# A graph network on one core: the convolutions of the last three or four target tiles are summed by gathers on Pool and adds on VectorE instead of by products with the adjacency table

## The chip, the cores and the metric

The kernel runs on one core of a Trainium2 chip. A time is the microseconds of one execution on the device. The engines of the core work side by side, each through its own queue of instructions, in the order of that queue: PE (matrix products), DVE (VectorE), ACT (ScalarE), POOL (GpSimd) and SP, which here only issues transfers. ACT and Pool issue transfers as well. An engine that must wait for another holds everything behind it in its queue.

## The reference

3125 nodes with 256 features and 50000 edges, sorted by target, pass through four blocks, each "x = x + layer(layernorm(x))" twice. What matters here are the two plain graph convolutions, the one of block 2 (three layers) and the one of block 3 (one layer):

```
def gcn_layer(h, src, dst, norm, n, W, b):          # block 2, with an edge from each node to itself
    h = h @ W
    msg = h[src] * norm[:, None]
    agg = segment_sum(msg, dst, num_segments=n)
    return agg + b
h = relu(gcn_layer(x, ..., W1, b1))
h = relu(gcn_layer(h, ..., W2, b2))
h = gcn_layer(h, ..., W3, b3)
...
h = x @ W                                            # block 3, one layer, no such edges
out = segment_sum(h[src] * norm[:, None], dst, num_segments=N)
```

with norm = d(src)^-1/2 · d(dst)^-1/2 and d the in-degree. After each convolution comes a mixture of 8 experts, of which every node takes the 2 best (hidden sizes 1024 in block 2, 512 in block 3). Blocks 0 and 1 are attention convolutions over the same edges, an expert stage and a recurrence with gates.

## The kernel before, in words

Nodes are cut into 25 tiles of 128 (NP = 3200 rows, the last ones empty); a node sits on a partition and its 256 features beside each other, and `x` stays on the core. Early in the program the edges are turned into a table of counts in DRAM, `ct16` [128, 25, 3200]: how often source row s·128+p has an edge to each target column. A convolution is then a dense product: for a group of target tiles (a span), SP loads the table's columns of these targets (`table_columns`, L814, tiles named `c`, three buffers), Pool adds the identity to the blocks on the diagonal where the layer has edges from each node to itself (L828, "own"), and PE multiplies, over all 25 source tiles, the source's rows by these columns.

The rows, `hs`, are f32 rows times d(src)^-1/2, cut into three bf16 parts (high, mid, low) so that three products with bf16 counts keep the precision. `parted` (L840) makes them, two tiles at a time: Pool casts (L847), DVE subtracts (L848), Pool casts (L849), DVE subtracts (L850).

`gcn` (L1585) runs a whole convolution. The first two layers of block 2 use `convolve` (L1529): 7 spans of 4, 4, 3, 4, 3, 4, 3 tiles, each 25 sources × 2 halves of the features × 3 parts = 150 matmuls (L1540), features on partitions and targets along the free axis, accumulated over two banks of PSUM, with two sets of banks. When a span ends, `done` runs: DVE multiplies the two banks by the targets' factor (`agg`, L1663), ACT applies bias and relu (L1664), PE multiplies each tile by the next layer's weights (L369, 4 matmuls a tile), ACT scales the result into `new` (L1656), and `parted` writes the next layer's `hs`. In PE's queue these products stand 9 matmuls into the next span.

The last layer of block 2 and the single layer of block 3 use `convolve_rows` (L1546): 13 spans of at most two tiles, rows of targets on partitions, for each tile and source one matmul 512 wide (high and mid, L1560) and one 256 wide (low, L1564). `done` here is `add`: DVE adds the scaled sums to `x` (L1684). Each finished span then passes through the front of the experts (`Experts.front`, L2198): normed rows on DVE, transposes and router product on PE, choice of two experts and places on DVE, and sends of the rows to the experts' slots by Pool (L2344, indirect transfers). These pieces are spread over the matmuls of the following spans by lags that are written out in `ready`, counted in tile-steps. When the convolution has ended, `Experts.run` (L2606) computes the experts; weights of the coming turn (`first`, L2599) are loaded by SP, `ahead` of them before the run starts.

The order in which instructions of different engines stand in the queues is not written out by hand: a scheduler places them from the order of the calls and its own view of when each can start. The order within a queue is fixed when the program is built.

Other names used below: `put_rows` (L834) stores rows of a tile in DRAM with a transfer issued by ACT; `even_spans` (L69) cuts a number of tiles into spans of nearly equal size; `recurrence` begins with a projection of all steps (L1801 with `px`, and DVE's L1824), about 66 us long, before the steps themselves. Attention convolutions gather rows with indirect transfers by Pool (L2019). If a flag is raised (`flags`), a general program runs after the normal one.

Of the kernel before, what the change touches and what calls it, by code (L numbers as in the profile page):

```python
# [19 lines left out]
P = 128  # L20
# [35 lines left out]
PARTS = 3  # L56
SKIP = 20
TOL = 2.0**-16
EPS = 1e-5
# [16 lines left out]
class Net:  # L76
    def __init__(self, ctx, tc, w, out):
# [11 lines left out]

        self.flags = const.tile([1, 7], F32, name="flags")  # L90
        nc.vector.memset(self.flags, 0.0)
# [30 lines left out]
        for g in range(QUAD):  # L122
            nc.vector.memset(self.quarter[g * GROUP : (g + 1) * GROUP, g : g + 1], 1.0)
        self.turned = dram.tile([GROUPED, MANY * P], BF16, name="turned")
        self.scored = [
            dram.tile([NP, D + 2 * nh], F32, name=f"scored{i}") for i, nh in enumerate((NH, NH, 1))
# [246 lines left out]
    def edges_by_window(self, ctx, c, keep):  # L373
# [10 lines left out]
        psum = self.pool(ctx, "tabps", 2, space=PSUM)  # L384
        dram = self.pool(ctx, "tabdram", 1, space=DRAM)
        edges = self.w["edges"]
# [3 lines left out]
        )  # L390
        runs = dram.tile([RUNS, 2 * P], I32, name="runs")
        nc.sync.dma_start(
# [178 lines left out]
    def count_degrees(self, ctx, c, psum):  # L571
# [53 lines left out]

        return [lambda q0=q0: some(q0) for q0 in range(0, HALF, quarter)] + [sums]

    def on_all_partitions(self, to, col, psum):
# [899 lines left out]

    def convolve(self, cpool, accp, loops, hs, done):  # L1529

        wide = 4
        for t0, n in even_spans(wide):
            cols = self.table_columns(cpool, t0, n, wide * P, loops)
            acc = [accp.tile([P, wide * P], F32, name=f"acc{f}") for f in range(KD)]
            for s in range(NT):
                parts = self.parts(hs, s)
                for f in range(KD):
                    for i, part in enumerate(parts):
                        lhs = part[:, f * P : (f + 1) * P]
                        self.nc.tensor.matmul(  # L1540
                            acc[f][:, : n * P], lhs, cols[s], start=(s == 0 and i == 0),
                            stop=(s == NT - 1), skip_group_check=True,
                        )
            done(t0, n, acc)

    def convolve_rows(self, cpool, accp, loops, hs, done, ready, loads):  # L1546

        nc = self.nc
        wide = 2
        step, waiting = 0, []  # L1550
        for t0, n in spans(wide):
            cols = self.table_columns(cpool, t0, n, wide * P, loops, few=4 * GRP // wide)
            acc = [accp.tile([P, 4 * P], F32, name=f"acc{t}") for t in range(n)]
            def add(t, lhs, s, start=False, stop=False):

                if len(hs.shape) == 3:
                    return nc.tensor.matmul(
                        acc[t][:, :D], lhs, hs[:, s, :], start=start, stop=stop
                    )
                nc.tensor.matmul(  # L1560
                    acc[t], lhs, hs[:, s, 0:2, :].rearrange("p i d -> p (i d)"), start=start,
                    stop=stop, skip_group_check=True,
                )
                return nc.tensor.matmul(  # L1564
                    acc[t][:, D:], lhs, hs[:, s, 2, :], start=False, stop=stop,
                    skip_group_check=True,
                )

            for s in range(NT):
                for t in range(n):  # L1570
                    add(t, cols[s][:, t * P : (t + 1) * P], s, s == 0, s == NT - 1)
                step += n
                while loads and loads[0][0] <= step:
                    with self.tc.issue_after(self.last_columns):
                        loads.pop(0)[1]()
                while waiting and waiting[0][0] <= step:
                    waiting.pop(0)[1]()
            for t in range(n):
                done(t0 + t, [acc[t][:, i * D : (i + 1) * D] for i in range(len(hs.shape) - 2)])
            for lag, piece in ready(t0, n):  # L1580
                waiting.append((step + lag, piece))
            waiting.sort(key=lambda entry: entry[0])
        return [piece for _, piece in loads + waiting]

    def gcn(self, name, weights, biases, loops, experts, split=True):  # L1585
# [3 lines left out]
        with ExitStack() as ctx:  # L1589
# [6 lines left out]
            accp = self.pool(held, name + "acc", 2, space=PSUM)  # L1596
            shape, kind = ([P, NT, PARTS, D], BF16) if split else ([P, NT, D], F32)
            inner = held.enter_context(ExitStack())
            wk = self.pool(inner, name + "work", 3)
            fresh = self.pool(inner, name + "fresh", 2)  # L1600
            lefts = self.pool(inner, name + "left", 2)
            if len(weights) > 1:
                other = self.pool(inner, name + "hs2", 1)
                aggs = self.pool(inner, name + "agg", 1)
            wts = [self.load_matrix(c, w, D) for w in weights]
            bs = [self.load(c, b, [P, KD]) for b in biases[:-1]]
            bias = self.load_row(c, biases[-1], D) if biases else None

# [13 lines left out]

            def rows_of(to, t0, n):

                if not split:
                    return to[:, t0 : t0 + n, :], lambda: None
                new = fresh.tile([P, 4, D], F32, name="new")[:, :n, :]

                return new, lambda: self.parted(lefts, to, new, t0, n)

# [6 lines left out]
            def use(t):  # L1637
                ph = psum.tile([P, 512], F32, name="tp")
                self.product(ph[:, :D], xts[t], wts[0])
                if t % 4 == 0:  # L1640
                    xts["new"] = rows_of(hs, t, min(4, NT - t))
                new, end = xts["new"]
                nc.scalar.mul(new[:, t % 4, :], ph[:, :D], disc[:, t : t + 1])
                if t % 4 == 3 or t == NT - 1:
                    end()
# [4 lines left out]
            for i in range(len(weights) - 1):  # L1650
                after = (other, last)[i].tile(shape, kind, name="hs")

                def next_layer(t, xt, to, i=i):
                    po = psum.tile([P, 512], F32, name="tp")
                    self.product(po[:, :D], xt, wts[i + 1])
                    nc.scalar.mul(to, po[:, :D], disc[:, t : t + 1])  # L1656

                def done(t0, n, acc, i=i, after=after, next_layer=next_layer):
                    w = n * P
                    agg = aggs.tile([P, KD, 4 * P], F32, name="agg")  # L1660
                    for f in range(KD):
                        a = agg[:, f, :w]
                        nc.vector.tensor_mul(a, acc[f][:, :w], dis[:, t0 * P : t0 * P + w])  # L1663
                        nc.scalar.activation(a, a, AF.Relu, bias=bs[i][:, f : f + 1])  # L1664
                    new, end = rows_of(after, t0, n)
                    for j in range(n):
                        next_layer(t0 + j, agg[:, :, j * P : (j + 1) * P], new[:, j, :])
                    end()
                    if i == 0:
                        some = x[:, t0 : t0 + n, :]  # L1670
                        nc.vector.tensor_add(
                            some, some, bias.unsqueeze(1).to_broadcast([P, n, D])
                        )

                self.convolve(cpool, accp, loops, hs, done)
                hs = after
# [16 lines left out]
            def ready(t0, n):  # L1693
                pieces = experts.front(psum, t0, n)
                if t0 + n == NT - 1:
                    lags = [1] + [16 + j for j in range(n)] + [20, 23, 25]
                else:
                    lags = [2] + [34 + 4 * j for j in range(n)] + [46, 58, 70]
                lags += lags[-1:] * (len(pieces) - len(lags))
                if t0 + n == CERTAIN:  # L1700
                    lags[-1] += 32
                return zip(lags, pieces)

            rest = self.convolve_rows(cpool, accp, loops, hs, add, ready, loads)
            held.close()
# [58 lines left out]
    def recurrence(self, name, general=False, turned=None):  # L1764
# [23 lines left out]
        with ExitStack() as ctx:  # L1788
# [18 lines left out]
            with ExitStack() as inner:  # L1807
                psz = self.pool(inner, name + "projpz", 4, space=PSUM)
                if xt is None:
# [4 lines left out]
                    for t in range(NT):  # L1814
                        xn = wk.tile([P, D], F32, name="xn")
                        self.normed(xn, x, stats, t)
                        self.transposed(psum, xt[:, :, t * P : (t + 1) * P], xn)
                steps = xt[:, :, :T].rearrange("p k (b g s) -> p k g s b", g=G, s=L)
                for g in range(G):
                    for s in range(L):  # L1820
                        pz = psz.tile([P, W], F32, name="px", padded_shape=[P, 512])
                        for k in range(KD):
                            quarters(pz, steps[:, k, g, s, :], us[:, k], k == 0, k == KD - 1)
                        nc.vector.tensor_add(pre[:, g, s, :], pz, bs)  # L1824
            with ExitStack() as inner:
                wk = self.pool(inner, name + "work", 3)
# [125 lines left out]
class GatheredAttention:  # L1952
# [143 lines left out]
    def end(self, t, state):  # L2096
        nh = self.nh
        acc = state["acc"][:, : D + 2 * nh].rearrange("p (h c) -> p h c", h=nh)
        for i, piece in enumerate(self.done(t, acc)):
            self.waiting.append((self.now + 4.0 * (i + 1), piece))  # L2100
        self.waiting.sort(key=lambda entry: entry[0])


# [660 lines left out]
def last_blocks(net, name):  # L2764

    with ExitStack() as part:
        f2 = Experts(
            net, part, "f2" + name, 1024, "L2_ffn_Wr", "L2_ffn_W1", "L2_ffn_b1", "L2_ffn_W2",
            "L2_ffn_b2", bias="L2_ffn_br", gain="L2_ffn_ln_g", shift="L2_ffn_ln_b",
            store=True, early=6, ahead=2, more=3,  # L2770
        )
# [40 lines left out]
def gnn_ffn_kernel(ctx: ExitStack, tc: tile.TileContext, w, out: bass.AP):  # L2812
    net = Net(ctx, tc, w, out)
    nc = tc.nc
    with ExitStack() as part:
        f0 = first_experts(net, part, "f0", early=10, ahead=1, more=4, late=3, rows=10)
        f0.run(rest=net.gnn0(f0))
    with ExitStack() as part:
        net.recurrence("l", turned=net.gnn1(part))
# [76 lines left out]
```

## Time and profile before

| what | value |
|---|---|
| median of 10 runs | 3951.31 us (3943.26 to 3958.70) |
| profiled execution, its own time | 3950.82 us |
| span of its trace | 3949.0 us, 71651 instructions |
| mean granted PE clock | 0.933 of full; 1.00 in the convolutions |
| PE busy | 3506.2 us, 89% of the span |
| convolutions of block 2, first two layers | 2325 to 2811 us; PE's idle time in 2330 to 2811 is 6.4 us |
| third layer of block 2 | 2811 to 3040 us |
| convolution of block 3 | 3480 to 3704 us |
| matmuls L1540 | 2100, 408.2 us |
| matmuls L1560 and L1564 | 1250 each, 411.3 and 340.8 us (they overlap) |

In lines of the profile, a time is the busy time in us, then the mean in ns, then the idle time of the engine ahead of such instructions with what ended it ("<-"). In a timeline the columns are the start, the length, and in brackets the idle time before and its releaser. PE's matmuls are pipelined, so lengths of neighbours overlap, and the step from one to the next is what counts. "L369" is the line of a helper that many products share; the names of the tiles tell them apart.

### The profile page before, as it was taken

The page shows a single profiled execution, that of the slowest core. Times are in us where ns is not written, and L with a number is a line of the kernel's source. Part 1 is how long each engine was busy: PE and PEld are TensorE (multiplying, and loading weights), DVE is VectorE, ACT ScalarE, POOL GpSimd, SP SyncE. Part 2 cuts the span into 40 slices and gives each one's busy share as a digit, 9 for nine tenths or more (in the row PEclk, how much of TensorE's full clock was granted, in tenths as well). Part 3 has the DMA queues.
Part 4 walks back from the last instruction along what each step waited for, and adds up shares of the span by engine and source line. Part 5 has one row for each costly group of instructions (what it writes and reads, how often), then busy time and mean ns, then how long its engine had stood idle before and what let it go on. Part 6 is the DMA issues. An engine that isn't in the chain of part 4 may idle for free. (4 is left out here: it accounts for less than half of the span.)

```text
span 3949.0 us, 71651 instructions
## 1 busy us (share of the span) xinstructions
PE 3506.2 (89%) x26079; PEld 2127.8 (54%) x26079; DVE 2155.4 (55%) x7897; ACT 1183.6 (30%) x3591; POOL 1422.8 (36%) x1321
## 2 busy tenths in 40 slices
PE   4777986867988798999999989999999999899897
PEld 3343222742322576744544555555566888766686
DVE  7777988547777575676766771111266211244411
ACT  2566334342343122133433450000001222320122
POOL 2778876446787474000000031111122222222243
PEclk8677988989999899999999989999999999899999
DMA  4556444644443553000000003233455344535465
GB/s 127 157 163 187 115 116 123 191 142 128 126 119 92 173 160 89 3 2 2 2 2 2 2 31 92 87 92 95 142 179 162 105 122 122 150 109 153 122 168 121
DMA packets 366366, 422.11 MB, mean 107 GB/s; under 512 B 44076, under 2 KB 320864, under 8 KB 362295
## 3 DMA queue, kind: packets, MB, share of 16 engines
q1 hardware_dynamic: 286833, 260.46, 21.9%
q0 software_dynamic: 62224, 140.41, 13.7%
q10 hardware_dynamic: 16950, 16.54, 1.3%
q8 instruction: 215, 3.52, 0.4%
q14 instruction: 144, 1.18, 0.1%
HBM read 337.37 MB, written 82.62 MB: 106 GB/s over the span
## 5 line engine op out<-in xcount | busy, mean ns | idle before, releaser
L2019 POOL DMA_INDIRECT edge<-scored,from x720 | 860.9, 1196 | 332.8 <-issue 180.1
L1560 PE MATMUL acc<-hs,c 128*128 128x512 bf16 x1250 | 411.3, 379 | 0.0
L1540 PE MATMUL acc<-c,hs 128*128 128x512 bf16 (+1 forms) x2100 | 408.2, 357 | 0.2 <-POOL hs L847 0.2
L1801 PE MATMUL pz<-lstm_v,hist 128*32 128x192 f32 x7120 | 384.2, 334 | 25.3 <-DVE hist L1902 7.0
L2685 PE MATMUL ph<-xt,first 128*128 128x256 f32 (+1 forms) x1624 | 349.2, 370 | 1.6 <-ACT xt L2651 1.0
L1564 PE MATMUL acc<-hs,c 128*128 128x256 bf16 x1250 | 340.8, 273 | 0.0
L2703 PE MATMUL py<-w,ht 128*128 x1484 | 336.2, 381 | 0.6 <-DVE y L2708 0.6
L2078 ACT ACTIVATE edge<-edge,factor 128x65 f32<-128x65 f32 (+1 forms) x960 | 251.3, 349 | 237.0 <-DVE factor L2073 220.9
L1540 PEld LDWEIGHTS <-hs 128*128 128x128 bf16 x2100 | 205.2, 98 | 199.5 <-POOL hs L847 0.6
L2685 PEld LDWEIGHTS ph<-xt,first 128*128 128x128 f32 x1624 | 290.3, 196 | 35.6 <-ACT xt L2651 1.6
L2703 PEld LDWEIGHTS py<-w,ht 128*128 128x128 f32 x1484 | 282.5, 191 | 38.3 <-issue 0.9
L1801 PEld LDWEIGHTS pz<-lstm_v,hist 128*32 128x32 f32 x7120 | 187.1, 110 | 178.6 <-DVE hist L1902 146.3
L1837 PE MATMUL pz<-pre,ident 128*128 128x192 f32 x900 | 269.4, 383 | 11.9 <-PEq L1910 11.4
L1611 POOL TENSOR_TENSOR disc<-deg,expo 128x25 f32<-128x25 f32 x1 | 4.4, 4356 | 727.4 <-DVE ends L1907 727.4
L2344 POOL DMA_INDIRECT slots<-rows,sloti x150 | 159.5, 1064 | 295.9 <-DVE rstd L345 136.5
L2693 ACT ACTIVATE ht<-ph,first 128x256 f32<-128x256 f32 (+1 forms) x406 | 160.5, 455 | 321.4 <-PE ph L2685 304.0
L976 DVE SCALAR_TENSOR_TENSOR v<-q,g1ahv,c 128x384 f32<-128x384 f32 (+1 forms) x400 | 236.8, 645 | 10.7 <-PE acc L1045 10.5
L1131 PE MATMUL acc<-g1bhv,v 128*128 128x257 f32 x850 | 206.7, 395 | 15.7 <-DVE v L976 8.5
L1837 PEld LDWEIGHTS pz<-pre,ident 128*128 128x128 f32 x900 | 136.7, 191 | 149.5 <-ACT tcell L1896 75.5
L1038 PE MATMUL acc<-v,g1ahv 128*64 128x384 f32 (+1 forms) x800 | 180.6, 560 | 28.8 <-DVE v L976 28.0
L1882 ACT ACTIVATE z<-pz 128x192 f32<-128x192 f32 x450 | 148.6, 330 | 189.7 <-PE pz L1801 175.5
L2088 PE MATMUL edgeacc<-edge,hot 128*32 128x264 f32 (+1 forms) x1440 | 141.6, 460 | 68.4 <-DVE edge L2081 34.7
(530 smaller groups left out, 5430.2 us busy)
## 6 DMA issues: line engine op xcount, KB each, us to landing
c<-ct SPq DMA_DIRECT2D x103, 640.0 KB
c<-ct SPq DMA_DIRECT2D x75, 480.0 KB
first<-in_f_first SPq DMA_DIRECT2D x29, 1158.0 KB
slots<-slots SPq DMA_DIRECT2D x159, 130.0 KB
ct<-cols SPq DMA_DIRECT2D x12, 1600.0 KB
first<-in_f_first SPq DMA_DIRECT2D x29, 642.0 KB
edge<-scored,from POOLq DMA_INDIRECT x720
first<-in_f_first SPq DMA_DIRECT2D x29, 385.0 KB
```

What stands on the lines that cost most here:

```text
L976: nc.vector.scalar_tensor_tensor(to, q[:, h, :w], hv[:, s, h, D // nh + 1 : D // nh + 2], cols[s], op0=ALU.max, op1=ALU.mult,)
L1038: made = nc.tensor.matmul(acc[h // 2][r : r + HC, :w], hv[:, s, h, :HC], v[h], start=first, stop=last, tile_position=(0, r),).ins
L1131: nc.tensor.matmul(a[:, : D + 1], v[0][:, j * P : (j + 1) * P], hv[:, s, 0, : D + 1], start=(s == 0), stop=(s == NT - 1),)
L1540: self.nc.tensor.matmul(acc[f][:, : n * P], lhs, cols[s], start=(s == 0 and i == 0), stop=(s == NT - 1), skip_group_check=True,)
L1560: nc.tensor.matmul(acc[t], lhs, hs[:, s, 0:2, :].rearrange("p i d -> p (i d)"), start=start, stop=stop, skip_group_check=True,)
L1564: return nc.tensor.matmul(acc[t][:, D:], lhs, hs[:, s, 2, :], start=False, stop=stop, skip_group_check=True,)
L1801: made = nc.tensor.matmul(pz[q * R : (q + 1) * R, :], s, m, start=start, stop=stop, tile_position=(0, q * R),)
L1837: made = nc.tensor.matmul(pz, self.ident, pre[:, g, s, :], start=True, stop=False)
L2019: nc.gpsimd.indirect_dma_start(out=tile[:, g, :], out_offset=None, in_=self.rows, in_offset=bass.IndirectOffsetOnAxis(ap=index, axis=0),)
L2078: nc.scalar.mul(part, part, factor[:, g, h : h + 1])
L2685: made = nc.tensor.matmul(ph[:, m - m0, :n, :], st["w1"][:, k * hid + m * P : k * hid + (m + 1) * P], st["xt"][:, k, :n, :], start=(k == 0 ...
L2703: nc.tensor.matmul(py[:, j, :], st["ht"][:, m, j, :], st["w2"][:, m * D : (m + 1) * D], start=(m == 0), stop=(m == nhc - 1),)
```

## The change

The last four target tiles (21 to 24; in `convolve_rows` the last three, 22 to 24) leave the dense product. `convolve` covers 21 tiles in 6 spans (4, 3, 4, 3, 4, 3) and `convolve_rows` 22 tiles in 11 spans of two. For the "near" tiles a target's edges are taken by rank: its first edge, its second, up to the 22nd. A table `ranked` holds for each target and rank the source row (or a row of zeros, if the target has fewer edges). For each rank Pool gathers, with one indirect transfer of 128 rows of 1 KB, the f32 source rows of the 128 targets; DVE adds two ranks at a time (128x512). Edges beyond rank 22, at most 128 for the four tiles together, are gathered once (`more`) and spread to their targets by one f32 product a tile with a table of ones, `beyond_hot`. The source rows lie in DRAM (`sources`, one copy for even and one for odd layers), written by `put_rows` when `new` is finished. More than 128 edges beyond the rank raise a flag.

The tables are made by `near_plan` in 16 pieces, some 70 small instructions, most on DVE, one piece after every fourth step of the recurrence's projection. The core of the diff:

```diff
+NEAR, RANKS = 4, 22
+FAR = NT - NEAR
...
+        self.sources = [dram.tile([NP + P, D], F32, name=f"sources{i}") for i in range(2)]
...
-    def convolve(self, cpool, accp, loops, hs, done):
+    def convolve(self, cpool, accp, loops, hs, done, near):
...
-        for t0, n in even_spans(wide):
+        for t0, n in even_spans(wide, FAR if near else NT):
...
+                if near:
+                    near.upto(n)
             done(t0, n, acc)
+        if near:
+            near.upto(None)
...
-        for t0, n in spans(wide):
+        for t0, n in even_spans(wide, near.first if near else NT):
...
+            for other in fronts.pop(t0 + n, ()) if near else ():
+                for lag, piece in ready(*other):
+                    waiting.append((step + 24 + lag, piece))
...
+            nears = self.pool(held, name + "near", 1) if split else None
+            gots = self.pool(held, name + "got", 5) if split else None
...
-                return new, lambda: self.parted(lefts, to, new, t0, n)
+                def end():
+                    self.put_rows(self.sources[layer % 2], new, t0, n)
+                    self.parted(lefts, to, new, t0, n)
+
+                return new, end
...
+                def near_done(t, rows, i=i, after=after, next_layer=next_layer):
+                    turned, agg = [], aggs.tile([P, KD, P], F32, name="nearagg")
+
+                    def turn():
+                        pt = psum.tile([P, KD, P], F32, name="tp", padded_shape=[P, 512 // P, P])
+                        for f in range(KD):
+                            nc.tensor.transpose(
+                                pt[:, f, :], rows[:, f * P : (f + 1) * P], self.ident
+                            )
+                        for f in range(KD):
+                            nc.scalar.activation(
+                                agg[:, f, :], pt[:, f, :], AF.Relu, bias=bs[i][:, f : f + 1]
+                            )
...
-                self.convolve(cpool, accp, loops, hs, done)
+                self.convolve(
+                    cpool, accp, loops, hs, done, near_tiles(i, FAR, 3.3, near_done)
+                )
...
-                if t0 + n == NT - 1:
+                if split and t0 + n == FAR - 1:
+                    lags = [2] + [22 + 4 * j for j in range(n)] + [34, 40, 46]
+                elif not split and t0 + n == NT - 1:
                     lags = [1] + [16 + j for j in range(n)] + [20, 23, 25]
...
-            rest = self.convolve_rows(cpool, accp, loops, hs, add, ready, loads)
+            rest = self.convolve_rows(
+                cpool, accp, loops, hs, add, ready, loads,
+                near_tiles(len(weights) - 1, FAR + 1, 3.9, near_add),
+                {12: [(FAR + 1, 2)], 18: [(FAR + 3, 1)]},
+            )
...
+                pieces = self.near_plan(inner) if turned else []
...
+                        if pieces and s % 4 == 3:
+                            pieces.pop(0)()
...
+class NearTiles:
+
+    def __init__(self, net, pool, gots, psum, rows, hs, disc, first, pace, done):
...
+        self.tiles = range(first, NT)
+        self.each = RANKS // 2
+        self.waiting, t0 = [], 7.0
+        for i, t in enumerate(self.tiles):
+            state, begin = {}, t0 + i * self.each * pace
+            self.put(begin, lambda t=t, state=state: self.begin(t, state))
+            for b in range(self.each):
+                at = begin + (b + 1) * pace
+                self.put(at, lambda t=t, b=b, state=state: self.add(t, b, state))
+            self.put(at + 0.1, lambda t=t, state=state: self.end(t, state))
+        self.more = pool.tile([P, D], F32, name="more")
+        self.gather(self.more, self.net.beyond)
+        self.fetch(5)
...
+    def fetch(self, upto):
+        for n in range(len(self.got), min(upto, len(self.tiles) * self.each)):
+            t, b = self.first + n // self.each, n % self.each
+            got = self.gots.tile([P, 2, D], F32, name="got")
+            for j in range(2):
+                r = 2 * b + j
+                self.gather(got[:, j, :], self.net.ranked[:, t - FAR, r : r + 1])
+            self.got.append(got)
+
+    def upto(self, n):
...
+        self.now += 0.325 * n
+        while self.waiting and self.waiting[0][0] <= self.now:
+            self.waiting.pop(0)[1]()
+
+    def begin(self, t, state):
...
+        nc.tensor.matmul(
+            pm[:, :D], self.net.beyond_hot[:, t - FAR, :], self.more, start=True, stop=True
+        )
...
+    def add(self, t, b, state):
+        n = (t - self.first) * self.each + b
+        if b == 0:
+            return
+        sums = state["sums"]
+        self.nc.vector.tensor_add(sums, self.got[n - 1] if b == 1 else sums, self.got[n])
+        self.fetch(n + 6)
...
-            store=True, early=6, ahead=2, more=3,
+            store=True, early=6, ahead=1, more=3,
```

`near_tiles` makes a `NearTiles` for a layer; in `upto` its pieces are called when the products written so far, at 0.325 us each, have come to their due time: the first at 7.0, then one add every 3.3 us (3.9 in `convolve_rows`). These due times order the calls; the scheduler places the instructions. `begin` also adds the tile's own three parts of `hs` where the layer has edges to itself; `end` adds the two halves of `sums` to `base` and scales; then `near_done` turns the tile, applies relu and multiplies by the next layer's weights, or `near_add` adds it to `x`. The weights of the convolutions move to a pool (`early`) that is freed before the last layer, and the second expert stage keeps one `first` load ahead where it kept two.

## Prediction

> **What bounds the kernel now.** I read the slices of the span first, to see which engine is full in the convolutions (slices 24 to 31 and 36 to 38).
>
> ```profile
> PE   4777986867988798999999989999999999899897
> DVE  7777988547777575676766771111266211244411
> POOL 2778876446787474000000031111122222222243
> PEclk8677988989999899999999989999999999899999
> ```
>
> PE is at 9 there, VectorE at 1 to 2, Pool at 1: the change moves work from the full engine to two that idle. The table of stretches says how full (columns: length, PE, weight loads, VectorE, ScalarE, Pool busy, granted clock, DMA share, GB/s); two stretches of the first two convolutions, two of the third, one of the fourth:
>
> ```profile
> 2400.00:2500.00 100.00, 99.99 (x502) 52.78 (x501) 12.84 (x19) 8.69 (x17) 10.46 (x20) 1.00 0.30 86
> 2700.00:2811.00 111.00, 110.99 (x586) 60.98 (x585) 12.59 (x19) 8.69 (x17) 12.30 (x24) 1.00 0.32 92
> 2811.00:2900.00 89.00, 88.99 (x566) 56.32 (x564) 45.02 (x262) 6.17 (x16) 17.66 (x24) 1.00 0.62 190
> 3480.00:3560.00 80.00, 80.00 (x510) 50.40 (x509) 33.60 (x156) 3.60 (x9) 16.28 (x21) 1.00 0.50 147
> ```
>
> PE never waits here, so products taken away shorten the span one for one, and a wait put on PE lengthens it one for one. The timeline shows one span's products and its handover; then the gathers that exist (groups, page):
>
> ```profile
> 2395.17 3.72 PE L369 MATMUL tp<-L_gnn_W,agg 128*128 128x256 f32 x16
> 2398.73 32.65 PE L1540 MATMUL acc<-c,hs 128*128 128x512 bf16 x152
> 2431.35 3.72 PE L369 MATMUL tp<-L_gnn_W,agg 128*128 128x256 f32 x16
> ```
>
> ```profile
> 2393.67 1.29 DVE L1663 TENSOR_TENSOR agg<-acc,dis 128x512 f32<-128x512 f32 x2 [25.78 <-PE acc L1540]
> 2398.39 0.69 DVE L848 TENSOR_TENSOR left<-new,hs 128x512 f32<-128x512 f32 x1 [3.42 <-POOL hs L847]
> ```
>
> ```profile
> L2019 POOL DMA_INDIRECT edge<-scored,from x720 | 860.9, 1196 | 332.8 <-issue 180.1
> L1560 PE MATMUL acc<-hs,c 128*128 128x512 bf16 x1250 | 411.3, 379 | 0.0
> L2344 POOL DMA_INDIRECT slots<-rows,sloti x150 | 159.5, 1064 | 295.9 <-DVE rstd L345 136.5
> ```
>
> ```profile
> 105.61 0.94 POOL L2019 DMA_INDIRECT edge<-scored,from  x1 [0.30 <-issue]
> ...
> 110.61 1.02 POOL L2019 DMA_INDIRECT edge<-scored,from  x1 [0.30 <-issue]
> ```
>
> ```profile
> 110.19 0.19 DVE L2073 TENSOR_TENSOR factor<-factor,edge 128x16 f32<-128x16 f32 x1 [3.50 <-DMA edge<-scored,from]
> ...
> 113.63 0.19 DVE L2073 TENSOR_TENSOR factor<-factor,edge 128x16 f32<-128x16 f32 x1 [1.67 <-DMA edge<-scored,from]
> ```
>
> A gather of 128 rows of 1 KB holds Pool 0.96 and the next starts 0.30 later: a step of **1.27 us** (0.95 plus 0.30 to 0.33 in the rows here; back-to-back L2019 steps have median 1.29, smallest 1.25, 95th percentile 2.26). Its rows are used 4.58 (105.61 to 110.19) and 3.02 us (110.61 to 113.63) after it started; I take 3.5.
>
> **What is removed.** A 512-wide step is 32.65 / 152 = 0.215 us, so 150 of them, one span, 32.2. Each of the first two convolutions has 25 tiles in spans 4, 4, 3, 4, 3, 4, 3 and afterwards 21 in 4, 3, 4, 3, 4, 3: one four-tile span less. The four `L369` products remain (3.72), one by one. Added on PE per tile are a 256-wide product (3.72 / 16 = 0.23) and two transposes (0.2 each at most): 0.6, times four 2.4. Net −30 each. A tile of the row-wise convolutions is 25 pairs of matmuls that start 0.326 us apart, 8.15 us; three tiles less their 0.23 each: −23.7 each. Removed: 2×30 + 2×23.7 = **107 us**. Column loads shrink too; nothing waits for them, 0.
>
> **What is added, and where it queues.** Per convolution one gather of `more`, then 22 gathers and 10 adds a tile: 89 gathers in the first two (113 us of Pool), 67 in the others (85). They would fit beside 205 us of products. But engines take instructions in order, and the changed program's order puts near work ahead of what PE needs. First convolution, counted in the built queues:
>
> ```
> Pool     more + 28 gathers, own block tile 4, 13 gathers, own 5 and 6, 13 gathers, ...
> VectorE  10 adds of tile 21, 9 of tile 22, agg of span 0 (L1904), 1 add, ...
>          next agg after 62 gathers, the third behind the cast after 81
> PE       9 products of span 1, then the L369 products of span 0
> ```
>
> So `agg` of span 0 waits for 43 gathers. The old kernel starts span 0's products at 2395.17; the last rows of `hs` exist near 2364, and a store must land before the first gather. Five bigger stores took 6.6 and 6.9 us until the following gather; I take 3.5 for one tile, so the first gather starts near 2368.5, and PE needs the products 26.6 us later. The 43rd gather starts 42×1.27 + 0.4 (own block, 31.2 / 75) ≈ 54, is usable at 58, the add takes 0.69, and products follow `agg` by 1.5 (2393.67 to 2395.17): 60.2. **PE stands 33.6.** VectorE then stands until 78.7 at tile 22's own product, which PE reaches only then; the five double buffers fill; gather 62 starts at 92.3, products go at 97.8 against PE's 89.7: 8.1 more. The third handover costs 4.7. Sum 46.4.
>
> Second convolution, same order, 44 gathers ahead, PE there at 29.7: 62.0 − 29.7 = 32.3, then 8.0, 4.7, and 0.5 for `more`: 45.5. Third (row-wise; front pieces of the experts queue on VectorE behind the adds): own block of span 1 after 15 gathers 5.5, normed rows after 32 gathers 17, selection after 44 gathers 10, the one after 62, behind eight slot sends, 8, `more` 1: 41.5. Fourth: no own blocks; normed rows after 22 gathers 7.5, selection after 42 (57.5 + 2 against 43) 16.8, the one after all 66 with eight sends between 9.5, `more` 1: 35. Stalls: **168 us**, about 286 s − 195 for a gather step of s us, since in each case the last checkpoint (81, 81, 62, 62 gathers) sets the total.
>
> Small ones. The plan of ranks adds 16 pieces to VectorE in the projection before the recurrence, where PE is full and VectorE idle in 30 of 66 us: between 0 (hidden) and 20 (every piece shown); I take 4. The second expert stage keeps one `first` load ahead instead of two: the load now starts at the convolution's end rather than 8 us ahead of its use; such loads landed in 5.7; between 0 and 8, I take 3. Stores of `sources` are 0.35 us ScalarE issues where ScalarE is 9% busy: 0, at most 2 a convolution.
>
> **Sum.** 3950.8 (profiled execution; span 3949.0; the median shown, 3951.3, is the same) − 107 + 168 + 7 = **4019 us**.
>
> [...] The gathers of this case step at 1.25 to 2.26 beside VectorE work. [...] The 704 steps have their median at 1.29, with VectorE 40 to 90% busy, so the sum stays with 1.27.
>
> **Rivals.**
> - *The gathers keep ahead (faster).* If the step is short enough, VectorE never waits and only the 107 show: 3951 − 107 + 7 = 3851. It decides at the first `agg`: 42 s + 6.1 ≤ 26.6, s ≤ 0.49; the gain ends where 286 s − 195 = 100, **s = 1.03**. Against it: no back-to-back step under 1.25 in 704. For it: those rows come from other stages and another row layout, and my walk assumes that every queued add blocks `agg`. Between 0.49 and 1.03 it ends at 3850 to 3950, say 3890.
> - *About even.* Half of the later stalls are not there (the second and third handovers, the sends), and the first ones are shorter because the first gather starts 6 us earlier: 168 − 35 − 24 = 109, 3960. Only a landing under 1 us with all later stalls gone gives within 8 us, which is 0.2%, about what can be told from no change.
> - *Worse.* Column loads (0.3 to 0.6 of the DMA engines) or the adds slow the step to 1.6: 286×0.33 = 94 more, 4113.
> - *It doesn't do what it says.* More than 128 edges beyond rank 22 would send the program to its general path. The drawn edges have 74 for the last four tiles (7159 edges, 437 targets): excluded.
>
> **Chances.** Forecast (3980 to 4060) 0.58; worse 0.14; partly refunded, 3959 to 3980, 0.07; even, within 0.2%, 0.05; faster 0.16. So slower 0.79, same 0.05, faster 0.16. The range leaves out a third of worse and nearly all of faster (0.05 + 0.14): 3935 to 4105. Bounds of the unknowns: landing 3.0 to 4.6 moves the sum by −2 to +4; steps 1.25 to 1.5, −6 to +66; first gather ±3 us, ∓12; the small ones −7 to +30.
>
> **What would show it.** In the changed profile the first two convolutions must have, some 34 us after their start, one PE gap of about 33 us ended by ScalarE or VectorE at the products of span 0, with VectorE waiting there for a gather by Pool; gathers stepping by 1.27 on Pool without pause for some 50 us; smaller gaps near the second and third handovers; and in the row-wise ones gaps of 17 and 10, and of 7 and 17, before the expert's transposes. Matmul busy time must fall by about 100. No gap at the first handover means the order did not bind; a step off 1.27 gives the total by 286 s − 195. I am wrong if PE stays full in these stages, or if gaps are ended by column loads instead.

## The result and the profile after

The changed kernel takes **4079.71 us** (median of 8 runs, 4075.52 to 4087.21), the one before 3951.26 (28 runs): a ratio of 1.0325, 95% interval 1.0316 to 1.0334. It is slower by 128 us, where 68 were forecast (4019); the direction held, and the time lies inside the range, near its upper end. In the profiled executions the span grows from 3949.0 to 4078.0.

The slices of the span of the changed kernel, rows as in those shown of before:

```profile
PE   4787886858987899999999868969699999768897
DVE  7787987457777566776676743222376211344511
POOL 2887865537884772000000164362632222363243
PEclk8777987979999999999999989979899999889999
```

PE's row of nines is broken: it is at 6 in slices 24, 27 and 29, where the three convolutions of block 2 begin, and at 7 and 6 in slices 35 and 36, where that of block 3 does. Pool is at 6 in slices 24, 27, 29 and 36, and the granted clock (PEclk) drops to 7 or 8 with PE. What PE waited for in the first two convolutions, in the third and in the fourth (the view of waits, its main lines; total us, times, longest):

```profile
PE tp L373 <- ACT agg L1905: 88.4, 8, 34.3
```

```profile
PE tp L2601 <- DVE sel L2592: 23.0, 4, 9.5
PE tp L356 <- DVE plain L2537: 14.6, 1, 14.6
PE tp L2414 <- DMA more<-sources,beyond: 4.1, 1, 4.1
PE acc L1758 <- POOL c L1022: 3.3, 1, 3.3
```

```profile
PE tp L2601 <- DVE sel L2592: 30.6, 5, 12.7
PE tp L356 <- DVE rows L2537: 15.3, 1, 15.3
```

Line 373 is the old 369, 1905 the relu behind `agg`, 2592 the choice of experts, 2537 the normed rows. The first pause in full, on PE, VectorE and Pool (timeline):

```profile
2401.69 3.35 PE L1734 MATMUL acc<-c,hs 128*128 128x512 bf16 x17
2439.39 5.51 PE L373 MATMUL tp<-L_gnn_W,agg 128*128 128x256 f32 x16 [34.34 <-ACT agg L1905]
```

```profile
2433.90 0.72 DVE L2431 TENSOR_TENSOR sums<-sums,got 128x512 f32<-128x512 f32 x1 [1.75 <-DMA got<-sources,ranked]
2437.29 0.69 DVE L2431 TENSOR_TENSOR sums<-sums,got 128x512 f32<-128x512 f32 x1 [2.67 <-DMA got<-sources,ranked]
2437.89 1.28 DVE L1904 TENSOR_TENSOR agg<-acc,dis 128x512 f32<-128x512 f32 x2
```

```profile
2432.28 0.95 POOL L2388 DMA_INDIRECT got<-sources,ranked  x1 [0.30 <-DVE sums L2431]
2433.24 0.81 POOL L1022 TENSOR_TENSOR c<-c,ident 128x128 bf16<-128x128 bf16 x2
2434.21 1.24 POOL L2388 DMA_INDIRECT got<-sources,ranked  x1 [0.16 <-issue]
```

PE stood for 34.34 us. VectorE held `agg` ready to run all that time, but had adds in front of it, each waiting 1.1 to 3.1 us for a gather (the last two are shown), and Pool issued gathers without rest but for three own blocks. This is the picture that the prediction asked for.

Sums by stage, from the same two traces. "Wait" is time in which no matmul runs; "half clock" is what matmuls of the convolutions and products lost by steps of 427 instead of 216 ns, of which more below.

| stage | before | after | change | wait | half clock |
|---|---|---|---|---|---|
| up to the first convolution | 2325.1 | 2335.5 | +10.4 | | |
| first two convolutions | 485.9 | 525.5 | +39.6 | 6.4 to 94.4 | 3.5 to 14.8 |
| third, to the experts' products | 230.1 | 267.7 | +37.6 | 2.7 to 49.0 | 0.3 to 13.2 |
| second experts' products | 380.5 | 379.1 | −1.4 | | |
| from them, with the fourth, to the next | 286.6 | 324.2 | +37.6 | 22.6 to 73.2 | 0 to 8.2 |
| third experts' products | 217.3 | 219.3 | +2.0 | | |

The half clock here is counted by steps. The profile's records of the granted clock, over the time in which PE worked, give a little more: 3.4 to 14.3, 0.4 to 14.9 and 5.0 to 14.2 us.

### The profile page after: what moved, and what is told of

Same layout as the page of the kernel before. It is cut to its first block, busy times and chain, and to the rows that moved or that the text cites. A ratio compares the mean times of both kernels' runs of the same rounds, so it can differ in the third digit from the quotient of the medians.

```text
span 4078.0 us, 71458 instructions
## 1 busy us (share of the span) xinstructions
PE 3441.6 (84%) x25545; PEld 2099.7 (51%) x25545; DVE 2276.1 (56%) x8175; ACT 1190.3 (29%) x3604; POOL 1739.7 (43%) x1640
## 5 line engine op out<-in xcount | busy, mean ns | idle before, releaser
L1758 PE MATMUL acc<-hs,c 128*128 128x512 bf16 x1100 | 383.7, 395 | 8.5 <-POOL hs L1043 5.2
L2388 POOL DMA_INDIRECT got<-sources,ranked x308 | 301.5, 979 | 154.8 <-issue 68.7
L1734 PE MATMUL acc<-c,hs 128*128 128x384 bf16 (+1 forms) x1800 | 348.8, 353 | 0.2 <-POOL hs L1041 0.2
L2337 ACT ACTIVATE edge<-edge,factor 128x65 f32<-128x65 f32 (+1 forms) x960 | 251.3, 349 | 242.4 <-DVE factor L2332 224.1
L1762 PE MATMUL acc<-hs,c 128*128 128x256 bf16 x1100 | 309.3, 281 | 0.5 <-DVE hs L1044 0.5
L1734 PEld LDWEIGHTS <-hs 128*128 128x128 bf16 x1800 | 176.4, 98 | 162.3 <-issue 1.6
L3065 POOL DMA_INDIRECT sums<-y,to x53 | 82.5, 1557 | 286.5 <-DVE y L3056 278.9
```

The source lines that it names most:

```text
L1734: self.nc.tensor.matmul(acc[f][:, : n * P], lhs, cols[s], start=(s == 0 and i == 0), stop=(s == NT - 1), skip_group_check=True,)
L1758: nc.tensor.matmul(acc[t], lhs, hs[:, s, 0:2, :].rearrange("p i d -> p (i d)"), start=start, stop=stop, skip_group_check=True,)
L1762: return nc.tensor.matmul(acc[t][:, D:], lhs, hs[:, s, 2, :], start=False, stop=stop, skip_group_check=True,)
L2337: nc.scalar.mul(part, part, factor[:, g, h : h + 1])
L2388: self.nc.gpsimd.indirect_dma_start(out=to, out_offset=None, in_=self.rows, in_offset=bass.IndirectOffsetOnAxis(ap=index, axis=0),)
```

## The experiments

The theory from the prediction: the near work costs time because of **where it stands in the queues** of VectorE and Pool; what waits for gathers holds up what PE needs. The rival: the gathers and adds cost the time **by themselves**, through traffic or engine time, in any order. A second question came from the half-clock column: what a pause of PE costs beyond its length. A time that is given without a ratio is that of one execution.

**First: held behind earlier work on VectorE.**

```diff
         while self.waiting and self.waiting[0][0] <= self.now:
-            self.waiting.pop(0)[1]()
+            self.held(self.waiting.pop(0)[1])
+
+    def held(self, piece):
+        traced, dve = self.nc.cur_bb.bb.instructions, self.nc.vector.engine
+        last = [i for i in traced[-700:] if i.engine == dve and i.name not in self.mine][-10:]
+        first = len(traced)
+        with ExitStack() as after:
+            for ins in last:
+                after.enter_context(self.net.tc.issue_after(ins))
+            piece()
+        self.mine.update(i.name for i in traced[first:])
```

> The changed kernel, with one thing added: every near piece that falls due while products are written is queued on VectorE behind the last ten VectorE instructions written before it that are not near work, so no add stands ahead of an earlier span's agg or an earlier front piece. In the built queues the first agg then stands behind 6 adds instead of 19, in the second layer behind 6 instead of 20; the gathers and adds are as many as before. Theory (order): the pauses of the changed profile, 88 us in the first two convolutions, 46 and 50 in the row-wise ones, nearly all go, and with them the stretches of half clock behind them (about 34 us of products at 427 instead of 216 ns a step): 4080 - 88 - 90 - 30 = 3870, to 3900 if the pauses at the first own block and at more stay. Rival (the work itself): 312 gathers, their traffic and the adds cost the time wherever they stand in the queue: 4050 to 4080.

Measured: 3924.93 us, ratio to before 0.9929 (0.9903 to 0.9955). The same gathers and adds, 155 us less than in the changed kernel. The rival falls. But it is 25 to 55 us short of the theory: what PE waited for in the first two convolutions is now

```profile
PE tp L373 <- ACT agg L1905: 11.7, 4, 7.4
PE acc L1734 <- POOL c L1022: 4.0, 2, 2.1
```

88.4 us have become 11.7. In the trace the longest of them comes from Pool: a cast of `hs` stands behind 16 gathers, VectorE's subtraction waits for it, and `agg` (at 2439.60) stands behind the subtraction:

```profile
2438.12 0.43 DVE L1042 TENSOR_TENSOR left<-new,hs 128x256 f32<-128x256 f32 x1 [8.77 <-POOL hs L1041]
```

**Second: adds that do not wait.**

```diff
-        self.nc.vector.tensor_add(sums, self.got[n - 1] if b == 1 else sums, self.got[n])
+        self.nc.vector.tensor_add(sums, self.still if b == 1 else sums, self.still)
```

> The changed kernel, but the adds read a tile of zeros that nothing else writes, so the sums of the near tiles leave out the gathered rows; all gathers are still made, into the same buffers, in Pool's queue as before. Theory (order on VectorE): the pauses that agg, plain and sel end go, while those that an own block on Pool ends may grow, since own blocks still stand behind 28, 40 and 41 gathers: of 184 us of pauses 100 to 160 go, 3910 to 3980. Rival (gathers slow PE by their traffic or their time on Pool, whoever waits): above 4040.

Measured: 4114.67 us, slower than the changed kernel and outside what my theory expected. Taken alone the number would speak for the rival; the waits of PE in the first two convolutions do not:

```profile
PE tp L373 <- ACT agg L1905: 80.4, 4, 46.3
PE acc L1734 <- POOL c L1022: 50.9, 4, 15.8
```

Without waiting adds the scheduler put 30 gathers in a row ahead of a cast; the own blocks (50.9 us) and the casts on Pool were late, and `agg` with them. So Pool's queue is a second place where the order binds, which I had priced only for own blocks and for single casts and sends. The experiment did not separate what it was meant to; the ninth repeats it in order.

**Third: tables alone.** `near_tiles` returns nothing and the lags are those of before:

```diff
-                ) if split else None
+                ) if False else None
```

> The changed kernel without near tiles: all 25 tiles go through the dense products with the spans and lags of before; the rank tables, the stores of the source rows and the single first load stay. It prices what is not the convolutions. My prediction had 7 us (4 for the tables, 3 for the load), the changed profile starts its first convolution 10.4 us later than the old one and ends its expert stages as early or as late within 2: 3958 to 3966. Rival (the 10 us are the scatter of one execution): within 0.2% of 3951.

Measured: 3944.00 us, ratio 0.9983 (0.9973 to 0.9994): not 7 us slower but 7 faster. Its first convolution begins 4.5 us later than before; the gain is in the stretch to the third expert stage's products (278.8 us for 286.6) and in these (211.3 for 217.3). Which part brings it (the weights' pool, the single `first` load) was not tried. Against this kernel the near tiles cost 136 us.

**Fourth: a pause of known length.** In the kernel before, PE's next span is queued behind the products of the finished one, and VectorE lengthens the handover:

```diff
+                        with self.tc.issue_after(turned) if turned else nullcontext():
...
                         nc.vector.tensor_mul(a, acc[f][:, :w], dis[:, t0 * P : t0 * P + w])
+                        for _ in range(24 if f == 0 else 0):
+                            nc.vector.tensor_scalar(a, a, 1.0, None, op0=ALU.mult)
```

> The kernel before, with PE made to pause: at each handover of a span in the first two convolutions VectorE multiplies the first half of agg 24 times by one, and PE's products of the next span are queued behind those of the finished one, which stand 0 matmuls instead of 9 into it; by the built queue 12 of 14 handovers pause. Theory (a pause of PE costs more than its length): 12 pauses of some 10 us, and behind each some 4 to 6 us of matmuls at 427 instead of 216 ns, 2 to 3 us lost each: 3951 + 120 + 30 = 4100. Rival (a pause costs its length alone): no 427 ns steps behind them and the sum of the pauses, 4070.

Measured: 4124.32 us. The first two convolutions grew by 172.7 us: 144.4 of pauses (12 of 12.0 on average, 10.6 to 12.7) and 25.8 of half clock, 2.2 for each (28.6 and 2.4 by the clock records). The timeline of the first, with the 16 matmuls behind it:

```profile
2408.30 5.16 PE L369 MATMUL tp<-L_gnn_W,agg 128*128 128x256 f32 x16 [12.50 <-ACT agg L1671]
2413.30 7.07 PE L1542 MATMUL acc<-c,hs 128*128 128x512 bf16 x32
```

The 16 took 5.16 us for the 3.72 of the kernel before. All twelve pauses show it: each, 12.0 us long on average, cost 14.2.

**Fifth: both queues held.** In addition to the first experiment, pieces are queued behind the last eight Pool instructions too, ScalarE casts, and the row-wise layers start later:

```diff
+        last += [i for i in others if i.engine == self.nc.gpsimd.engine][-8:]
...
-                    self.parted(lefts, to, new, t0, n)
+                    self.parted(lefts, to, new, t0, n, nc.scalar.copy if layer else None)
...
-        self.waiting, t0 = [], 7.0
+        self.waiting, t0 = [], 12.0 if self.adding else 7.0
...
-        self.fetch(5)
+        self.fetch(3 if self.adding else 5)
```

> The first experiment taken further: near pieces are queued behind the last ten VectorE and the last eight Pool instructions written before them that are not near work; in the first two convolutions the casts of hs for the next layer are made by ScalarE instead of Pool, so that none stands behind gathers; in the row-wise ones the first pieces fall due at 12 instead of 7 us and six gathers instead of ten are issued at once, so that the first own block stands behind 7 gathers. The first experiment left 23 us of pauses in the first two convolutions and 28 and 33 in the two others (22 of the 33 are also in the kernel before, ahead of its products), each pause ended by a cast, an own block, more or the normed rows, and 20 us of slow products. Theory (order in both queues): most of these go, 3925 - 15 - 25 - 10 = 3875, between 3860 and 3895. Rival (what is left is the time that the gathers and adds take from others): 3910 to 3930.

Measured: **3879.64 us**, ratio to before 0.9823 (0.9805 to 0.9841), the fastest version of this study. The first two convolutions take 424.3 us for 485.9, 61.6 less, with 6.1 us of waits. The products of the handover, in these two convolutions, in the changed kernel and in this one (groups):

```profile
L373 PE MATMUL tp<-L_gnn_W,agg 128*128 128x256 f32 x156 | 49.4, 481 | 88.4 <-ACT agg L1905 88.4
```

```profile
L373 PE MATMUL tp<-L_gnn_W,agg 128*128 128x256 f32 x156 | 36.7, 387 | 0.0
```

The same 156 matmuls: 88.4 us of waiting and 12.7 of half clock are gone. Whether the hold on Pool or ScalarE's casts did it, on top of the first experiment, was not tried apart. The row-wise convolutions gain little: 230.3 us, where the kernel with the tables alone has 230.5, and 274.9 for its 278.8.

**Sixth and eleventh: short pauses.** The fourth experiment without multiplications (sixth), and with 3 of them (eleventh).

> The fourth experiment without the multiplications by one: 12 handovers at which PE's next span is queued behind the products of the finished one, nothing else. There 12 pauses of 12.0 us cost 12 x 12.0 of waiting and 12 x 2.2 of products at half the clock. The multiplications took some 8.5 us of each, so 12 pauses of about 3.5 us are left. Theory (half a clock for some us follows a pause of 3.5 us as well as one of 12): 3951 + 42 + 26 = 4019. Rival (a short pause costs its length alone): 3951 + 42 = 3993.

> The sixth experiment with 3 multiplications by one. 24 of them made a pause 11.1 us longer (12.0 against 0.9), 0.46 each, so 12 pauses of about 2.3 us. Pauses of 0.9 us had no products at half the clock behind them, pauses of 3.3 us and more in the changed kernel had them for 4 to 6 us. If half the clock follows a pause of 2.3 us too: 3951 + 28 + 26 = 4005. If not: 3951 + 28 = 3979.

Measured: 3959.18 and 3990.67 us. The pauses of the sixth were 0.9 us, not 3.5 as expected, and cost their length: the two convolutions grew by 10.6 us with 10.2 more of waits, and no more half clock than before. In the eleventh, two pauses that follow one another:

```profile
2438.79 5.41 PE L369 MATMUL tp<-L_gnn_W,agg 128*128 128x256 f32 x16 [2.79 <-ACT agg L1671]
2444.03 24.54 PE L1542 MATMUL acc<-c,hs 128*128 128x384 bf16 x150
2470.93 2.86 PE L369 MATMUL tp<-L_gnn_W,agg 128*128 128x256 f32 x12 [2.35 <-ACT agg L1671]
```

16 matmuls in 5.41 us behind a pause of 2.79, 12 in 2.86 behind one of 2.35. Of its twelve pauses, three of the eight of 2.8 us had half clock behind them, none of the four of 2.35. Neither of the two expectations holds for all of them. Nor do these four set a border at 2.35 us. In the changed kernel's own fourth convolution PE works, stands for 2.29 us, works 1.7 us at the full clock and then 3.4 at half (table of stretches, columns as in the prediction):

```profile
3760.00:3762.30 2.30, 0.01 (x1) 0.00 (x0) 0.84 (x5) 0.00 (x0) 0.00 (x0) 1.00 0.06 20
3764.00:3767.40 3.40, 3.40 (x14) 1.78 (x12) 0.42 (x5) 0.63 (x2) 2.10 (x3) 0.50 0.11 39
```

A pause of 2.25 us in the same stage (at 3660.6) has none behind it, and one of 3.36 in the first experiment (at 2809.9) has none either. In the changed kernel's four convolutions all 13 pauses of 3.59 us or more have half clock in them or behind them, and so have the twelve of the fourth experiment. Of the shorter ones down to some 2 us some have it and some have not; in the first convolution of the kernel before, pauses of 2.08 and 2.10 us have it and one of 1.97 has not.

**Seventh: near tiles in the first two convolutions alone** (`near` is None in `convolve_rows`, with the lags of before).

> The fifth experiment with near tiles in the first two convolutions alone; the two row-wise ones go through all 25 tiles by products, with the lags of before. In the fifth the first two convolutions took 424 us for 486, the third 230 for 230, and the stretch from the second to the third expert stage's products 275 against 279 in the kernel with the tables alone. Theory (the row-wise convolutions give their 24 us of products back in pauses and slow products): 3944 - 61 = 3883, within 8 us of the fifth experiment's 3880. Rival (the row-wise ones do gain their 24 us each): 3880 + 48 = 3928.

Measured: 3891.70 us, ratio 0.9850 (0.9834 to 0.9867); 12 us above the fifth, where 8 were allowed and 48 would have been the rival's. The row-wise convolutions take 230.8 and 278.0 us here, 230.3 and 274.9 there, 3.6 us of the 12: their gain on PE is given back almost whole.

**Eighth: a slower pace in the row-wise layers.**

```diff
-                near_tiles(len(weights) - 1, FAR + 1, 3.9, near_add),
-                {12: [(FAR + 1, 2)], 18: [(FAR + 3, 1)]},
+                near_tiles(len(weights) - 1, FAR + 1, 4.3, near_add),
+                {14: [(FAR + 1, 2)], 18: [(FAR + 3, 1)]},
```

> The fifth experiment with the row-wise near adds due every 4.3 instead of 3.9 us, and the front of tiles 22 and 23 after the span that ends at tile 14 instead of 12. In the fifth, PE still waited there 13.5 us for sel, which stood behind adds whose gathers stood behind the sends of a span. Theory (order again: more room between gathers lets sends and gathers pass): 5 to 20 us less, 3860 to 3875. Rival (the Pool has too little time for gathers and sends in these stages in any order): 3880 or more.

Measured: 3893.64 us, 14 us slower than the fifth. The theory's 5 to 20 us of gain did not come; the third convolution waits 23.7 us instead of 20.3 and takes 236.5 instead of 230.3. A slower pace with a later front does not help; which of the two costs the time was not tried apart.

**Ninth: the second experiment in the mended order.**

> The fifth experiment, but the adds read a tile of zeros, so the gathered rows are left out of the sums while all gathers are made: the second experiment in the mended order. Theory (the second one's loss came from Pool's order, not from the gathers as such): 3945 - 61 for the first two convolutions, less 20 to 30 in the row-wise ones: 3845 to 3875. Rival (gathers cost PE time even if nobody waits): 3900 or more.

Measured: 3881.54 us; between the two expectations, above mine. The first two convolutions take 425.9 us, as in the fifth (424.3): there, gathers that nobody waits for and gathers that are waited for cost the same, nothing. The third takes 224.1 instead of 230.3, so waits of the adds are only 6 us of what is lost in it. Of the 24 us of products removed there, 6.4 are gained here against the kernel with the tables alone (230.5); 12 go to waits (15.9 for 3.5, for `sel` above all) and 5 to half clock. What holds `sel` up when no add waits stays open.

**Tenth: ScalarE's casts alone**, in the changed kernel's order.

> The changed kernel with one part of the fifth experiment alone: the casts of hs in the first two convolutions go to ScalarE. By the built queues VectorE's order stays as in the changed kernel: the first agg behind 19 adds, the second layer's behind 20. Theory (VectorE's order is the first cause, Pool's casts only the next one): the pauses of 34 and 32 us at the first handovers stay, 4050 to 4080. Rival (the casts behind gathers on Pool are the cause, the adds in front of agg are not): those pauses go, below 4010.

Measured: 4070.14 us. The pauses at the first handovers stay, 34.5 and 32.0 us:

```profile
PE tp L373 <- ACT agg L1906: 81.6, 6, 34.5
```

So VectorE's order was the first cause and Pool's the next one behind it. Mending the casts alone took 10 us off, mending VectorE's order alone 155, and mending Pool's as well another 45.

## Why the prediction was right, and where it fell short

- **What binds.** Right, shown by the first, fifth and tenth experiments: the order of the queues, `agg` behind adds that wait for gathers. One premise was read too widely: VectorE is at 1 to 2 in the first two convolutions only. In the slices that the prediction shows it is at 6 in the third and at 4 in the fourth (142 of 230 and 101 of 226 us busy), and in these two the near tiles gained at most some 6 us in any experiment.
- **The step of a gather.** Right: 1.25 us median in the changed profile (mean 1.32 of 299 steps within a run) for 1.27 taken. At the first handover the products start 60.0 us after the first gather (2379.39 to 2439.39), where the walk had 60.2. By 286 s − 195 the mean would give 182 us of waits, near the 185 measured; but a slower step would lengthen the waits everywhere, and those of the first two convolutions came out shorter than predicted (88.0 for 91.9).
- **Pauses.** Right in place and nearly in size. First convolution 33.6, 8.1, 4.7 predicted, 34.3, 7.8, 2.0 measured; second 32.3, 8.0, 4.7 against 32.2, 7.7, 2.0. Third 17, 10, 8, 5.5 and 1 against 14.6, 9.4, 9.5, 3.3 and 4.1. Fourth 7.5, 16.8, 9.5 against 15.3, 12.3, 12.7. In all, waits grew by 88.0, 46.3 and 50.6 us, 185 where 168 (and 3 for the experts' start) stood; most of the difference is the fourth, where I took its normed rows to wait for 22 gathers and had the least of the walk worked out; 5.2 us of waits stand ahead of its first gather, at a late cast on Pool that the walk did not have (the kernel before waited 2.5 there).
- **Products removed.** Right in itself: 61.6 us less in the fifth experiment's first two convolutions for 60. In the changed kernel only 48.4 of busy time went there.
- **The step that failed**, in the prediction's words: "a wait put on PE lengthens it one for one". In the changed kernel matmuls ran at half the clock for 3 to 6 us behind every pause of 3.3 us or more, and behind some shorter ones. That is 11.3 + 12.9 + 8.2 = **32 us** (35 by the clock records) that had no term in the sum. Rows that show it stood in the profile of before, and I read them as full clock in the convolutions and no more: PEclk is 6 to 8 in slices in which PE waits, and the stretch in which the first convolution begins, with three pauses of about 2 us, has a clock of 0.95:

```profile
2325.00:2400.00 75.00, 68.62 (x329) 43.63 (x330) 35.53 (x69) 31.40 (x76) 25.26 (x36) 0.95 0.15 45
```

The table of stretches of the changed profile, right behind the 34 us pause (same columns as in the prediction):

```profile
2439.00:2441.00 2.00, 1.61 (x4) 1.34 (x5) 0.87 (x2) 0.95 (x2) 1.39 (x3) 0.50 0.29 88
2441.00:2443.00 2.00, 2.00 (x7) 1.55 (x6) 0.00 (x0) 0.47 (x1) 1.65 (x2) 0.50 0.45 131
2443.00:2445.00 2.00, 2.00 (x11) 1.64 (x10) 0.00 (x0) 1.01 (x3) 1.44 (x2) 0.99 0.30 80
2445.00:2447.00 2.00, 2.00 (x14) 1.17 (x12) 0.00 (x0) 0.41 (x1) 1.40 (x2) 1.00 0.53 157
```

The clock is 0.50 for 4 us and then 0.99 and 1.00. The 16 products that begin there take 5.51 us, where the kernel before took 3.72. Pauses of 2.8 us (three of eight, eleventh experiment) and one of 2.29 were enough for such a stretch too. What sets it off, and why some of the short pauses have it and others have not, the runs do not show.

- **The small ones.** Wrong in sign: 7 us for tables and loads, where the third experiment measured −7. The 10.4 us ahead of the first convolution are not a fixed price of the tables: in single executions the other kernels with the tables begin it 3.1 to 12.3 us later than the kernel before (the second experiment 24), those without 1.8 to 2.9.

Together: 17 of waits less the 3 for the start, 32 of half clock and 6 ahead of the convolutions are 52 of the 61 us that the forecast was short of the profiled executions. Some 4 lie in and behind the experts' stages, and 5 in the products: by the stages' sums 102 us of them went, not 107 (105, if the clock records' 35 is taken for half clock).

That the time still lay in the stated range is in part luck: it reached up to 4105 mainly for a slower gather, which did not come, and had no term for the clock.

The rival "worse", a gather step of 1.6 through column loads or adds, came close in number (4113) and was wrong in its mechanism: the step in the changed profile was 1.25 us (median). The rival "the gathers keep ahead" was wrong for this kernel; what it says of the first two convolutions, products gone and nothing waiting, is what the fifth experiment shows there (61.6 us less), not by faster gathers but by adds that stand later.

## What to carry to other kernels

Before idle engines are given work, read in which order it lands in their queues: an instruction that waits for a slow transfer holds everything behind it, and PE pays if an evacuation is among that (34.34 us at the first handover here). Count how many transfers stand ahead of each instruction that the full engine needs, multiply by the step of one, and add what a pause of PE costs beyond its length: by the clock records another 1.7 to 3.0 us for each of the 13 of 3.59 us or more in the changed kernel's convolutions, 2.4 on average in the fourth experiment, and 1.7 behind the two of 2.08 and 2.10 us in the kernel before. When the order is the fault, tie the new work behind the old in each queue that both share; mending one queue alone can leave the time nearly as it was (4070 for 4080 in the tenth experiment).

## What the runs showed of the hardware that was not expected

After the pauses of PE of 3.59 us or more in the changed kernel's convolutions (13 of 13), granted clock 0.50 over 3.4 to 6.1 us of PE's work: steps of 427 for 216 ns (512 columns) and 213 for 109 (256 columns). None behind pauses of 0.9 us (12 of 12, sixth experiment). In between some had it: none at 2.35 (4 of 4, eleventh experiment) and at one of 3.36 (first experiment), but three in eight at 2.8 (eleventh) and the one at 2.29 in the changed kernel, each time for 3.41 us. Gathers of 128 rows of 1 KB by Pool cost a full PE no time that these runs show where it does not wait for them: the first two convolutions took 424.3 us in the fifth experiment and 425.9 in the ninth with 178 gathers each time, where 61 fewer than the 485.9 of before are the products themselves.
